# Ordering the start of a four-layer image kernel: the image first, the normalisation as a hand-ordered pipeline, constants and the second image's offsets inside the first gather

## Chip, cores and metric

The kernel runs on one NeuronCore of a Trainium2 chip. The metric is the device time of one execution in microseconds (us); lower is better. All data are float32.

## What is computed

Four layers work one after the other on four images of 192 channels and 64 by 64 pixels. The change concerns the first layer, which, cut to the part that matters, is

```
xn   = layernorm over channels of x            # 192 channels, 4096 pixels
off  = conv3x3(xn, w_p) + b_p                  # 18 offsets for each pixel: 9 taps, x and y
px, py = pixel + tap + off, clipped to the padded image (66 x 66)
xo   = bilinear sample of xn at (px, py)       # 4 neighbours, for 9 taps
att  = channel attention (per head) of conv(xo, w_d)   # its matrices are folded into one 192x192 matrix, m2
x    = x + m2 . xn ;   x = x + mlp(layernorm(x))
```

The second layer is a non-local block over the 4096 pixels, the third is windowed attention with an mlp, the fourth a small depthwise filter.

## The kernel before

All four images go through the same stages. For image b the first layer has three of them.

`offsets(b)` (from line 321) loads the image in eight chunks of 512 pixels (`xi`, L346) and normalises each with the helper `layer_norm_steps` (L271 to L303): mean on TensorE (`pm_l`, L277), difference on VectorE (`d_l`, L281), square on ScalarE (`sq_l`, L284), variance on TensorE (`pv_l`, L256), root on ScalarE (`r_l`, L289), reciprocal on VectorE (L291), spread back over pixels on TensorE (`pb_l`, L265), two products on VectorE (L301) and two affine steps on ScalarE into the padded image `xn` (L302). The helper is a generator, so that a caller can place its steps. Then the 33 tiles of 128 padded pixels are transposed (L372) and copied (`tt`, L373), and each group of 11 tiles is written four times, shifted, into a table in DRAM (`table<-tt`, L376), so that one table row of 3 KB holds a pixel's four neighbours. `xn` itself is written to DRAM too (`xnd`, L379). The 3x3 convolution of `xn` (`po`, L388) runs in three blocks of 4, 4 and 3 groups of 384 pixels, and twelve VectorE steps turn its result into weights and indices (`pos`, `fr`, `idx`, L400 to L417).

`gather(b)` (from L423) is a generator of 297 steps, one for each tile and tap. GpSimd issues an indirect DMA of 128 table rows into one of 11 slots (`ring`, L467); ScalarE and VectorE blend the four neighbours (`row`, `xo`, L473 to L478); TensorE multiplies the result with a tile of `xn` that SyncE loads from the table (`ti`, L463) into the sums `h` (L485). Some twelve short steps on small matrices follow (L501 to L570) and give `m2`. The gather needs the whole table of its image and all of `idx`.

`mlp0(b)` (from L573) reads the image and `xnd` again and applies `m2` and the mlp (L594 to L627).

The order of the stages: constants, `offsets(0)`, `gather(0)`, `offsets(1)`, `mlp0(0)`. Then for each image b come `keys(b)` (L649, eight chunks: load `xk`, two products `tp` L658 and `g` L663) and the second layer `layer1(b)`, with `gather(b+1)` woven into it, and the other layers, with `mlp0(b+1)` woven into them. For b of 1 and 2, `offsets(b+1)` stands between the chunks of `keys(b)`: after each of its eight norms it calls for one chunk.

The constants (L86 to L231) are loaded and prepared ahead of everything else: 48 small copies for one bias table (L141), two weight matrices that are read, scaled and written back to DRAM (`folded`, L181 to L199), and others.

The order on each engine comes from the framework: its scheduler takes the instructions in program order as priority, and lets a later one go ahead where it models it to be ready earlier. Inside `with tc.manual_schedule()` the program order is kept on each engine and on the DMA queue instead. The order is fixed when the program is built; at run time every engine works strictly in order. SBUF that a closed pool held is taken over by later pools, whose first writer waits until the last user is done.

Of the kernel before, what the change touches and what calls it, by code (L numbers as in the profile page):

```python
# [10 lines left out]
F32 = mybir.dt.float32  # L11
# [58 lines left out]
def conv_seq_kernel(ctx: ExitStack, tc: tile.TileContext, a, out: bass.AP):  # L70
# [25 lines left out]
    n128 = sum(m * n for _, m, n in _V128)  # L96
    v128 = load("v128", [128, n128], a["v128"])
    at = 0
    for name, m, n in _V128:
        V[name] = v128[:, at : at + m * n].rearrange("p (m n) -> p m n", m=m)  # L100
        at += m * n

# [14 lines left out]

    thetaT, phiT, gT = halves("thetaT"), halves("phiT"), halves("gT")
    wW = load("wW", [P, C], a["wW"])


    qkvT = const([P + 1, 2, 3 * C], "qkvT")
    nc.sync.dma_start(out=qkvT[:P], in_=a["qkvT"].rearrange("(k p) n -> p k n", p=P))
    nc.sync.dma_start(out=qkvT[P : P + 1, 1, :], in_=a["qkvb"])

    bias = const([128, 3, 2, WS * WS], "bias")


    N1 = 2 * WS - 1
    with tc.tile_pool(name="rpb", bufs=1) as rp:  # L130
        shifted = rp.tile([WS, HEADS, N1 * N1], F32, tag="shifted", name="shifted")
        n = N1 * N1 - WS + 1
        for iy in range(WS):
            nc.sync.dma_start(
                out=shifted[iy : iy + 1, :, 0:n],
                in_=a["rpb"][:, WS - 1 - iy : WS - 1 - iy + n].unsqueeze(0),
            )
        for e in range(HEADS):
            for ix in range(WS):
                rows = shifted[:, e, :].rearrange("p (r c) -> p r c", c=N1)[:, WS - 1 - ix : 2 * WS - 1 - ix, 0:WS]  # L140
                nc.sync.dma_start(out=bias[WS * ix : WS * ix + WS, e % 3, e // 3, :], in_=rows)  # L141
    nc.sync.dma_start(out=bias[64:128], in_=bias[0:64])

    v48 = load("v48", [48, 4], a["v48"])
# [22 lines left out]
    headsel = const([128, 2, P], "headsel")  # L167
    nc.gpsimd.memset(headsel, 0.0)
    for h in range(2):
        for e in range(3):  # L170
            row = P + 2 * e + h
            nc.sync.dma_start(out=headsel[row : row + 1, h, bass.ts(e, 32)], in_=ones[0:1, 0:32])


    sel6 = const([128, 32], "sel6")
    for c in range(0, 32, HEADS):
        n = min(HEADS, 32 - c)
        nc.sync.dma_start(out=sel6[P : P + HEADS, c : c + n], in_=ident[0:HEADS, 0:n])


    def folded(name, gamma, beta, bias_):  # L181

        n = a[name].shape[1]
        to = dram.tile([P, 2, n], F32, tag=f"scaled_{name}", name=f"scaled_{name}")
        b2 = const([128, n // 128], f"bias_{name}")
        with tc.tile_pool(name="fold", bufs=1) as fp, tc.tile_pool(name="foldps", bufs=1, space=PSUM) as pp:
            w = fp.tile([P, 2, n], F32, tag="w", name=f"w_{name}")
            nc.sync.dma_start(out=w, in_=a[name].rearrange("(k p) n -> p k n", p=P))
            p = pp.tile([128, n // 128], F32, tag="p", name=f"p_{name}")
            for m in range(n // 128):  # L190
                for k in range(2):
                    nc.tensor.matmul(
                        p[:, m : m + 1], lhsT=w[:, k, bass.ts(m, 128)], rhs=beta[:, k], start=k == 0, stop=k == 1
                    )
            nc.vector.tensor_tensor(b2, p, bias_.rearrange("p m n -> p (m n)"), ALU.add)
            for k in range(2):
                nc.vector.tensor_scalar_mul(w[:, k, :], w[:, k, :], gamma[:, k])
            nc.sync.dma_start(out=to, in_=w)
        return to, b2  # L199

    fc1_dram, fc1_bias = folded("fc1", V["l0_g2"], V["l0_b2"], V["l0_bfc1"])
    fc1b_dram, fc1b_bias = folded("fc1T", V["l2_n2g"], V["l2_n2b"], V["l2_fc1b"])
    with tc.tile_pool(name="foldq", bufs=1, space=PSUM) as pp:
        p = pp.tile([128, 2, 512], F32, tag="p", name="p_qkv")
        n = 3 * C // 2
        for u in range(2):
            for k in range(2):
                nc.tensor.matmul(
                    p[P : P + 1, u, 0:n], lhsT=V["l2_n1b"][:, k], rhs=qkvT[:P, k, bass.ts(u, n)], start=k == 0, stop=k == 1
                )  # L210
        row = qkvT[P : P + 1, 1, :].rearrange("p (u n) -> p u n", u=2)
        nc.vector.tensor_tensor(row, row, p[P : P + 1, :, 0:n], ALU.add)
        for k in range(2):
            nc.vector.tensor_scalar_mul(qkvT[:P, k, :], qkvT[:P, k, :], V["l2_n1g"][:, k])
# [9 lines left out]


    outb = const([P, 2], "outb")
    with tc.tile_pool(name="outb", bufs=1, space=PSUM) as pp:
        p = pp.tile([P, 2], F32, tag="outb", name="pob")
        for h in range(2):
            nc.tensor.matmul(p[:, h : h + 1], lhsT=wW[:, bass.ts(h, P)], rhs=V["l1_gb"], start=True, stop=True)  # L230
        nc.vector.tensor_tensor(outb, p, V["l1_Wb"].rearrange("p k n -> p (k n)"), ALU.add)  # L231
# [37 lines left out]
    MEAN, DIFFERENCE, SQUARE, VARIANCE, INVERSE = range(5)  # L269

    def layer_norm_steps(src, n, dst, sb, ps, name, affine=None, rows=None, tag="v", bufs=2, own=""):  # L271
# [21 lines left out]
        pb = spread_quarters(r, n, P, ps, name)  # L293
        for k in range(2):
            of, to, r = d[:, k, :], dst[:, k] if rows else dst[:, k, :], pb
            if rows:
                of, r = (t.rearrange("p (r c) -> p r c", r=rows) for t in (of, r))
            if affine is None:
                nc.vector.tensor_tensor(to, of, r, ALU.mult)  # L299
            else:  # L300
                nc.vector.tensor_tensor(of, of, r, ALU.mult)  # L301
                nc.scalar.activation(to, of, AF.Identity, bias=affine[1][:, k], scale=affine[0][:, k])  # L302
        return dst  # L303

    def links(steps, upto=None):

        while True:
            try:
                if next(steps) == upto:
                    return None  # L310
            except StopIteration as end:
                return end.value
# [8 lines left out]
    def offsets(b, pool, beside=None):  # L321
# [18 lines left out]
        with ExitStack() as s:  # L340
# [3 lines left out]
            for i in range(NCH):  # L344
                xi = sb.tile([P, 2, CN], F32, tag="xi", name=f"xi_{b}_{i}")
                nc.sync.dma_start(out=xi, in_=given(b)[:, :, bass.ts(i, CN)])  # L346
                layer_norm(
                    xi, CN, xnv[:, :, 1 + 8 * i : 9 + 8 * i, 1:65], sb, ps, f"l0_{b}_{i}",
                    affine=(V["l0_g1"], V["l0_b1"]), rows=8,
                )  # L350
                if beside is not None:
                    beside()

            wp = s1.tile([P, 2, 9, 32], F32, tag="wp", name=f"wp_{b}")
            nc.gpsimd.memset(wp, 0.0)
            for k in range(2):
                nc.sync.dma_start(out=wp[:, k, :, 0:18], in_=a["wp"][P * k : P * k + P])
            bp = s1.tile([128, 1], F32, tag="bp", name=f"bp_{b}")
            nc.gpsimd.memset(bp, 0.0)
            for q in range(4):  # L360
                nc.sync.dma_start(out=bp[32 * q : 32 * q + 18, :], in_=a["bp"])
            p0 = s1.tile([128, NT, 18], F32, tag="p0", name=f"p0_{b}")
            nc.sync.dma_start(out=p0, in_=a["p0"])

            G, T = 11, 3
            for g in range(NT // G):
                tt = sb.tile([128, G, C], F32, tag="tt", name=f"tt_{b}_{g}")
                for j in range(G):
                    t0 = (g * G + j) * 128 + MID
# [3 lines left out]
                    nc.scalar.copy(tt[:, j, :], pt)  # L373
                for q in range(4):
                    e = g * G * 128 + (2 - q // 2) * WP + 2 - q % 2
                    nc.sync.dma_start(  # L376
                        out=table[e : e + G * 128, bass.ts(q, C)].rearrange("(j p) c -> p j c", p=128), in_=tt
                    )
            nc.sync.dma_start(out=xn_drams[b % 2], in_=xn)  # L379
            for g0 in range(0, NT // T, 4):  # L380
# [3 lines left out]
                for tap in range(9):  # L384
                    for k in range(2):
                        for q in range(ng):
# [4 lines left out]
                            )  # L391
                ot = sb.tile([128, T * 128], F32, tag="ot", name=f"ot_{b}_{g0}")
# [10 lines left out]
                )  # L403

# [15 lines left out]
    def gather(b, s, at, m2):  # L420
# [8 lines left out]
        wkT, wvT, wv, wprojT = (halves(n, keep) for n in ("wkT", "wvT", "wv", "wprojT"))  # L429

        def long(name):

            n = a[name].shape[1]
            lo, hi = (keep.tile([128, n], F32, tag=f"{name}_{i}", name=f"{name}_{i}_{b}") for i in range(2))
            nc.sync.dma_start(out=lo, in_=a[name][64:C])
            nc.sync.dma_start(out=hi[64:128], in_=a[name][0:64])
            return lo, hi

        wk_long, wv_long = long("wkT"), long("wvT")

        wd = keep.tile([128, 14, C], F32, tag="wd", name=f"wd_{b}")
# [1107 lines left out]
```

## Time and profile before

| | |
|---|---|
| time, median of 3 runs | 7646.15 us (7644.78 to 7667.4) |
| time of the profiled execution | 7584.17 us |
| its span | 7582.4 us |
| mean granted TensorE clock | 0.914 |
| TensorE busy | 6609.8 us (87%) |
| VectorE, ScalarE, GpSimd busy | 68%, 49%, 27% |
| constants until the first norm's matmul | 0 to 87.6 us |
| first gather: first and last indirect DMA issued | 191.2 and 614.5 us |
| first matmul of the first image's mlp (`h`, L620) | 726.1 us |
| second layer's first score (`s`, L710) for images 1 and 2 (0 is the first) | 2776.4 and 4544.6 us |

Times in views of the profile are microseconds from the start of the span. A window's row gives, for each engine, its busy time and instruction count, then the granted TensorE clock as a part of full speed, the busy share of the 16 DMA engines, and the GB/s that they moved. In a timeline and in the chain of waits a row is start, duration, and what it was; "<-" stands between what is written and what is read; "SPq" is a DMA issue on SyncE's queue, and an entry "x4" merges four.

### The profile page before, as it was taken

The page shows a single profiled execution, that of the slowest core. Times are in us where ns is not written, and L with a number is a line of the kernel's source. Part 1 is how long each engine was busy: PE and PEld are TensorE (multiplying, and loading weights), DVE is VectorE, ACT ScalarE, POOL GpSimd, SP SyncE. Part 2 cuts the span into 40 slices and gives each one's busy share as a digit, 9 for nine tenths or more (in the row PEclk, how much of TensorE's full clock was granted, in tenths as well). Part 3 has the DMA queues.
Part 4 walks back from the last instruction along what each step waited for, and adds up shares of the span by engine and source line. Part 5 has one row for each costly group of instructions (what it writes and reads, how often), then busy time and mean ns, then how long its engine had stood idle before and what let it go on. Part 6 is the DMA issues. An engine that isn't in the chain of part 4 may idle for free.

```text
span 7582.4 us, 114456 instructions
## 1 busy us (share of the span) xinstructions
PE 6609.8 (87%) x44384; PEld 4281.5 (56%) x44384; DVE 5137.6 (68%) x7998; ACT 3717.0 (49%) x6080; POOL 2084.8 (27%) x2305
## 2 busy tenths in 40 slices
PE   5678999999978789998978879998987879989875
PEld 2455378885534358886634347886643447766432
DVE  2673269974677849994585748995576767755666
ACT  1673258864433248884543327884543325545331
POOL 0671047742100017771200006773210000012100
PEclk9879979997989889998989989998998979999987
DMA  4996147741000166761010056673010010010000
GB/s 136 310 335 211 40 153 222 218 154 33 23 24 13 31 199 216 221 211 50 9 32 17 13 157 218 211 221 110 12 27 22 11 43 11 13 33 10 6 0 18
DMA packets 373069, 756.61 MB, mean 100 GB/s; under 512 B 50999, under 2 KB 253287, under 8 KB 372142
## 3 DMA queue, kind: packets, MB, share of 16 engines
q0 software_dynamic: 95040, 467.22, 19.0%
q1 hardware_dynamic: 277486, 282.08, 12.8%
q8 instruction: 350, 5.73, 0.3%
q14 instruction: 193, 1.58, 0.1%
HBM read 642.66 MB, written 106.21 MB: 99 GB/s over the span
## 4 chain that ended last, share of the span: by engine, by line
PE 69%; DVE 15%; DMA 6%; ACT 5%; issue 2%; SPq 2%; POOL 1%; ACTq 0%; DVEq 0%; POOLq 0%
PE s L710 11%; PE y L776 9%; PE h L485 6%; PE h L1215 5%; PE o L626 3%; PE h L620 3%; DVE ha L1121 3%; PE v L936 3%; DVE ga L1121 2%; DMA ring<-table,idx 2%; PE f L1264 2%; PE qk L861 2%; PE t L944 2%; PE qk L862 2%; PE pm_l2n L277 1%
## 5 line engine op out<-in xcount | busy, mean ns | idle before, releaser
L467 POOL DMA_INDIRECT ring<-table,idx x1188 | 1685.3, 1419 | 1122.4 <-DMA table<-tt 280.5
L710 PE MATMUL s<-ths,ph 96*128 96x256 f32 x4096 | 982.4, 386 | 5.0 <-ACT ths L704 4.0
L710 PEld LDWEIGHTS s<-ths,ph 96*128 96x128 f32 x4096 | 785.6, 193 | 144.1 <-ACT ths L704 17.0
L473 ACT ACTIVATE row<-ring,pos 128x384 f32<-128x384 f32 x1188 | 698.8, 610 | 263.2 <-DVE xo L478 186.2
L485 PE MATMUL h<-ti,xo 128*128 128x192 f32 x3168 | 694.0, 354 | 148.7 <-DVE xo L478 58.5
L474 DVE SCALAR_TENSOR_TENSOR row<-ring,fr,row 128x384 f32<-128x384 f32 x1188 | 699.9, 613 | 122.2 <-ACT row L473 113.3
L776 PE MATMUL y<-sc,gx 128*97 128x256 f32 x3008 | 723.3, 379 | 0.0
L485 PEld LDWEIGHTS h<-ti,xo 128*128 128x128 f32 x3168 | 571.0, 204 | 256.0 <-DVE xo L478 142.3
L1121 DVE SCALAR_TENSOR_TENSOR ga<-gate,v,ga 128x512 f32<-128x512 f32 x720 | 541.4, 752 | 27.6 <-POOL gate L1095 0.2
L776 PEld LDWEIGHTS y<-sc,gx 128*97 128x97 f32 x3008 | 489.6, 164 | 123.3 <-issue 1.1
L477 ACT ACTIVATE xo<-row,pos 128x192 f32<-128x192 f32 x1188 | 505.4, 448 | 76.7 <-PE h L485 60.6
L478 DVE SCALAR_TENSOR_TENSOR xo<-row,fr,xo 128x192 f32<-128x192 f32 x1188 | 465.3, 411 | 55.2 <-ACT xo L477 52.0
L773 DVE TENSOR_TENSOR sc<-sc,mbs 128x1024 f32<-128x1024 f32 x376 | 448.6, 1217 | 12.8 <-ACT mbs L736 12.4
L712 ACT COPY sc<-s 128x1024 f32<-128x1024 f32 x376 | 377.2, 1003 | 158.4 <-PE s L710 157.7
L620 PE MATMUL h<-d_l0m,fc 96*128 96x512 f32 x768 | 375.4, 642 | 86.7 <-DVE d_l0m L299 86.7
L717 DVE TENSOR_TENSOR top<-top,sc 128x1024 f32<-128x1024 f32 x282 | 344.6, 1222 | 127.3 <-ACT sc L712 127.2
L774 ACT ACTIVATE sc<-sc 128x1024 f32<-128x1024 f32 x376 | 393.1, 1054 | 30.5 <-DVE sc L773 28.1
L1095 POOL COPY gate<-gate 128x192 f32<-128x192 f32 x28 | 15.3, 545 | 1397.1 <-ACT gate L1246 1397.1
L920 DVE TENSOR_REDUCE es<-ex 128x6 f32<-128x384 f32 x264 | 133.2, 546 | 391.7 <-ACT ex L916 391.7
L626 PE MATMUL o<-gl,fc 128*96 128x512 f32 x768 | 372.8, 637 | 0.0
L1215 PE MATMUL h<-d_l2n,fc1T 96*128 96x512 f32 x768 | 358.2, 615 | 14.5 <-ACT z L1218 7.8
L620 PEld LDWEIGHTS h<-d_l0m,fc 96*128 96x128 f32 x768 | 157.6, 207 | 294.5 <-issue 186.4
(308 smaller groups left out, 11178.5 us busy)
## 6 DMA issues: line engine op xcount, KB each, us to landing
table<-tt SPq DMA_DIRECT2D x48, 1056.0 KB
ti<-table SPq DMA_DIRECT2D x528, 96.0 KB
ring<-table,idx POOLq DMA_INDIRECT x1188, 5.2
xnd<-xn SPq DMA_DIRECT2D x4, 3270.0 KB
xo<-table SPq DMA_DIRECT2D x132, 96.0 KB
xb<-xnd SPq DMA_DIRECT2D x32, 396.0 KB
xi<-in_x_dram SPq DMA_DIRECT2D x32, 384.0 KB
xa<-in_x_dram SPq DMA_DIRECT2D x32, 384.0 KB
```

The costliest lines, as they stand in the source:

```text
L467: nc.gpsimd.indirect_dma_start(out=gt.rearrange("p r q c -> p (r q c)"), out_offset=None, in_=table[:, :], in_offset=bass.IndirectOffsetOn ...
L473: nc.scalar.activation(row, gt[:, :, 0, :], AF.Copy, scale=pos[:, t, 9 + tap : 10 + tap])
L474: nc.vector.scalar_tensor_tensor(row, gt[:, :, 1, :], fr[:, t, 9 + tap : 10 + tap], row, ALU.mult, ALU.add)
L477: nc.scalar.activation(xo[:, j, :], row[:, 0, :], AF.Copy, scale=pos[:, t, tap : tap + 1])
L478: nc.vector.scalar_tensor_tensor(xo[:, j, :], row[:, 1, :], fr[:, t, tap : tap + 1], xo[:, j, :], ALU.mult, ALU.add)
L485: nc.tensor.matmul(acc[m // 2][:, bass.ts(m % 2, C)], lhsT=xo.rearrange("p j c -> p (j c)")[:, bass.ts(m, 128)], rhs=tt, start=t == 0 and ...
L620: nc.tensor.matmul(p, lhsT=fc1[:, k, bass.ts(m, 128)], rhs=hn[:, k, :], start=k == 0, stop=k == 1)
L626: nc.tensor.matmul(p, lhsT=fc2[:, m, bass.ts(h, P)], rhs=gl[:, m, :], start=m == 0, stop=m == 5)
L710: nc.tensor.matmul(p[:, t, :], lhsT=ph[:, bass.ts(G * g + t, 128)], rhs=ths[i], start=True, stop=True)
L776: nc.tensor.matmul(py, lhsT=gx[:, G * g + t, :], rhs=ex[:, t, :], start=g == 0 and t == 0, stop=g == NG - 1 and t == G - 1,)
L1121: nc.vector.scalar_tensor_tensor(to, src(tap), w[:, k, tap : tap + 1], last, ALU.mult, ALU.add)
L1215: nc.tensor.matmul(p, lhsT=fc1b[:, k, bass.ts(m, 128)], rhs=hns[i][:, k, :], start=k == 0, stop=k == 1)
```

## The change

It has four parts.

1. The constants become a generator `constants()` of eleven yields. Only one small vector table, the identity and a few filled tiles stay in front.
2. `offsets` becomes a generator. For images 0, 2 and 3 it runs in a hand-written order in which the steps of chunk i+1 and chunk i alternate, transposes follow two chunks behind the mean, a third of the first convolution block is placed in each of three steps, and the other two blocks come last; `xnd` is written behind the table's last part. The two products of a norm become one instruction over 1024 elements.
3. While `gather(0)` runs, from its step 30 on, every fourth step takes one part of `constants()`, and after these every sixth step one part of `offsets(1)`, which is left to the scheduler. The loads of the gather's weights move behind its first 66 steps.
4. `keys(1)` and `keys(2)` give one chunk at each yield of `offsets`, which has two yields in each step of its pipeline.

```diff
-    (constants: v128, thetaT, phiT, gT, wW, qkvT, bias, v48, headsel, sel6, folded x2, outb: straight code)
+    def constants():
+        nonlocal thetaT, phiT, ...
+        (the same code, with a yield behind wW, behind each of the six heads of bias, behind headsel,
+         and around each of the two folded())
...
+        if affine is not None:
+            nc.vector.tensor_tensor(d, d, pb.unsqueeze(1).to_broadcast([P, 2, n]), ALU.mult)
+            yield PRODUCT
         for k in range(2):
...
-                nc.vector.tensor_tensor(of, of, r, ALU.mult)
                 nc.scalar.activation(to, of, AF.Identity, bias=affine[1][:, k], scale=affine[0][:, k])
...
+            def ready(i):
+                return NT if i == NCH else max(0, (8 * i + 1) * WP - MID) // 128
+            with ExitStack() as order:
+                if not woven:
+                    order.enter_context(tc.manual_schedule())
+                load(0)
+                load(1)
+                load_weights()
+                norm(0, SQUARE)
+                first = convolve(0)
+                for i in range(NCH + 1):
+                    if i + 2 < NCH:
+                        load(i + 2)
+                    norm(i + 1, MEAN)
+                    norm(i, VARIANCE)
+                    norm(i + 1, DIFFERENCE)
+                    norm(i, INVERSE)
+                    norm(i + 1, SQUARE)
+                    norm(i - 1)
+                    yield
+                    transposes(range(ready(i - 1), ready(i)))
+                    if i >= 5:
+                        next(first, None)
+                    norm(i, PRODUCT)
+                    yield
+                nc.sync.dma_start(out=xn_drams[b % 2], in_=xn)
+                links(first)
+                for g0 in (4, 8):
+                    for _ in convolve(g0):
+                        yield
...
-        for _ in gather(0, s, offsets(0, sb), m2):
-            pass
-        at = offsets(1, second)
+        at = links(offsets(0, sb))
+        beside = [constants(), offsets(1, second, woven=True)]
+        for k, _ in enumerate(gather(0, s, at, m2)):
+            if k < 30 or not beside:
+                continue
+            if len(beside) == 2 and k % 4 == 0 or len(beside) == 1 and k % 6 == 0:
+                try:
+                    next(beside[0])
...
                 if 0 < b < B - 1:
-                    at = offsets(b + 1, sb, lambda: next(making, None))
+                    parts = offsets(b + 1, sb)
+                    try:
+                        while True:
+                            next(parts)
+                            next(making, None)
```

`load`, `load_weights`, `norm(i, upto)`, `transposes` and `convolve` hold the code of before in functions; `convolve` yields after every three taps, and the difference tile `d_l` has three buffers instead of two.

## Prediction

> **What bounds the kernel now.** I read the page first, then the windows, then the chain of waits and the timelines of the three places that the diff touches: the start, the first gather with what follows it, and the offsets of images 2 and 3 beside the keys of images 1 and 2. Everything after the first score of each image's second layer keeps its code, so I sum only up to that point.
>
> Windows of the start and of the first gather:
>
> ```profile
> core 0: us, PE busy (x) PEld busy (x) DVE busy (x) ACT busy (x) POOL busy (x), PEclk, DMA share, GB/s
> 0.00:88.00 88.00, 15.71 (x61) 12.35 (x62) 4.36 (x10) 1.28 (x1) 5.64 (x33) 1.00 0.26 57
> 300.00:400.00 100.00, 72.92 (x344) 52.59 (x342) 83.11 (x171) 81.75 (x173) 75.61 (x73) 0.87 0.95 331
> 2640.00:2666.00 26.00, 24.45 (x75) 15.18 (x74) 16.65 (x20) 2.73 (x4) 0.00 (x0) 0.52 0.38 117
> ```
>
> For 88 us nothing is busy: the constants pass one by one through SyncE's queue. The gather is different: no engine is full, but the DMA engines are, at 0.95.
>
> Chain of waits, start and end of that part:
>
> ```profile
> 55.55 5.17 DMA w_fc<-in_fc_dram
> 87.58 3.71 PE pm_l L277 x4
> ...
> 180.32 9.71 DMA table<-tt
> ...
> 678.51 11.79 PE po L388 x144
> 691.51 11.78 PE po L388 x108
> ```
>
> The first norm begins at 87.58, the table lands at 190.03, the gather starts at 191.2. Behind it the second image's last two convolution blocks stand in the path, 678.5 to 703.3.
>
> Issues of SyncE's queue where image 2's offsets begin, and the DMA view of 190 to 610:
>
> ```profile
> 2634.24 1.22 SPq L655 DMA_DIRECT2D xk<-xd  x2
> 2653.66 8.46 SPq L655 DMA_DIRECT2D xk<-xd  x2
> 2662.18 0.59 SPq L1370 DMA_DIRECT2D out_dram<-out  x1
> 2667.90 0.82 SPq L346 DMA_DIRECT2D xi<-in_x_dram  x2
> DMA packets 49582, 135.27 MB, mean 322 GB/s; under 512 B 7369, under 2 KB 29311, under 8 KB 49550
> ```
>
> The image's first chunk is issued only when the last output of the image before has landed (2662.18 and 5.59, the chain's row for that transfer, make 2667.77): it takes over its SBUF. Key chunks need no such wait and fill TensorE from 2638.66 on.
>
> **First gather's start.** The first `xi` load goes out at about 1.2 instead of 56.0 and lands 5 later (the chain's 5.17 at 2668.28): TensorE starts at 6. The pipeline's step is a loop through three engines, since ScalarE must square chunk i+1 before it may write chunk i-1, whose transposes TensorE then awaits: means 1.72, difference 1.22, square 1.06, two affine steps 1.52, four transposes behind their copies 1.25, spread 1.11, six hand-offs 0.3: 8.2 us. That is what a chunk takes now (126.0 to 134.2), with convolution in its gaps. Chunks before, with few convolution matmuls beside them, took 9.4 (108.1 to 117.5). I take 9.0. The one product of 1024 elements, 1.22 by the difference's row against 1.28 for the two it replaces, gives nothing. The sum: first chunk, cold and with its activation table load, 12.8 (87.6 to 99.7 now, and a slow second mean); four steps of 9.0; three steps of 8.2 with a third of a block, 3.9, in them, 36.4; last product, affine steps, five transposes and an eviction 5.5; two blocks of 11.8 with their evictions 24.9; three adds and nine index instructions with hand-offs 6.9 (2763.5 to 2770.3 for image 2 now). Together 122.5; the gather can start at 129 (126 to 140), 62 earlier. Its table, written from about 97 on with 20 us for the last part (165 to 190 now), comes before that.
>
> **First gather's length.** By the trace it issues its last gather at 614.5, and its products go on up to 633; I take 632 as its natural end, since image 1's transposes and convolution, placed ahead of the last twelve products, hold these until 650.8. The whole DMA load moved inside now is 12 table writes of 1056 KB (13.0 MB), `xnd` 3.3, and constants of 3.3 (four transfers of 576 KB, 432, four of 72, smaller ones) with position tables 0.4: 20 MB, at 322 GB/s 62 us. Nothing hides it, as the share is 0.95 already. Beside it SyncE's queue gets about 85 small issues of 0.7, eight bias copies (5.5 us) for every four gather steps (5.5 us at 1.37 each), and table writes that hold the queue (18.3 us for four at 165.0); `ti` loads queue behind them, and TensorE's `h` behind those. The ring's 11 slots cover 15 us. I take 20 for what is left, ends 0 and 45. The moved weights cost the same bytes. So the last products end at 129 + (632 - 191) + 62 + 20 = 652.
>
> **Behind it.** The small matrices take 27.4 now (651.5 to 678.9), of which 5.5 are image 1's: 22. The mlp's loads are now hidden by the convolution that goes away: about 3 of issue and 5 of landing become visible, and from the first `m2` product (704.9) to the first `h` of the mlp (726.3) it is 21.4 as before. 652 + 22 + 8 + 21.4 = 703.4, against 726.3: **23 earlier** (ends, with the start at 126 to 140 and the weave at 0 to 45: 46 earlier, 13 later). The 25 us of convolution that leave the path give back only part: the loads and first norm of the mlp are late next.
>
> **Images 2 and 3.** Here the hand-written order adds a wait. Queued on TensorE behind the first mean are all eight key chunks; on SyncE `xk` stands behind the third `xi` load, which awaits the first difference. Now five and a half chunks run before the first mean (2673.5), in a time when TensorE has nothing else. After the change TensorE idles there. The last output instruction ends at 2656.1; without `xk` ahead of it its store lands at 2661.7, and `xi` at 2667. From there: first step 19 (the first difference ends 5 behind `xi`, `xk` lands 4 later, two key chunks of 3.64, the first slow, 8.9, spread 1.1); three steps of 8.2 less the 3.3 idle now filled, plus 7.3 of keys, 12.2 each, 36.6; one of 9; three with convolution 36.4; then 5.5, 24.9 and 6.9 as above; 6.1 from the index to the first score (2770.3 to 2776.4). 144.4: the score starts at 2811.4, not 2776.4, **35 later**. For image 3 the same with 4417.65, so `xi` at 4428.5: 4572.9 against 4544.6, **28 later**. Ends for both together: if `xi` need not wait and goes out with `xk` (2634.2, 4395.8, and 5.2 to land), 7 and 1; if it comes when it does now (2673.5, 4440.1), 42 and 40. I take 63, since the conflict is in the trace twice and the pool of `xi` becomes larger, not smaller.
>
> On the clock: 2640 to 2666 TensorE was 94% busy at a granted 0.52, and at 2666 it had full speed. The Trainium skill ("TensorE: Matmul & The Clock Gate", What's actually happening) says full rate comes after about 3.4 us of sustained work. By the rule my first steps are short enough as they stand; by the row the half clock could go on for 26 us and each of the two stages would be about 8 longer.
>
> **Sum.** 63 - 23 = 40 later. The profiled execution took 7584.2 with its span of 7582.4, so 7624 in its terms. The median of the runs shown is 62 above it; in the runs' terms 7646 + 40 = **7686**.
>
> **Rivals.** (1) *The loads are not held.* If the other SBUF layout lets `xi` go out with `xk`, images 2 and 3 lose 8 together, and with a clean weave (0 instead of 20) the first part gains 43: 35 faster, 7611. It decides as soon as the two stages cost less than the start gives. For it: weights and biases (L357 to L363) are in SBUF at 2616 already. Against: two of two waits. (2) *The moved bytes are hidden.* If the first gather were bound by VectorE and ScalarE (0.83 and 0.82 at 300 to 400), 62 would vanish and the 20 with them: 42 faster, 7604. Against: from 400 to 600, with those at 0.66 to 0.74, the pace is 1.31, hardly less than 1.37, and the DMA share the same. (3) *The weave stalls the gather.* Each load behind a blocked SyncE queue comes late, and a matmul on image 1 that awaits one blocks `h`, as for 39.9 us once at the start (wait of `h` for `xi`). If a third of 24 parts lose 8 us, it is 44 more: 84 slower, 7730. (4) *It does not do what it says:* the scheduler is free for image 1 and may push its parts behind the gather again, as now. Then the start gains its 62, the tail stays, the constants' 3.7 MB add 11, and the two stages 63: 12 slower, 7658.
>
> **Chances.** Forecast, including (4), 0.58, spread over +5 to +75 us; 0.11 of it within 0.3%, that is 23 us, about what a measurement of this kernel can tell from no change. Rival (1) 0.27, 0.24 of it faster by more. Rival (2) 0.08, faster. Rival (3) 0.07, slower. So faster 0.32, same 0.14, slower 0.54. The range reaches below rivals (1) and (2), and up to the forecast with the upper ends of the two stages (82 instead of 63), the weave (45) and the start (140): 7600 to 7740. The forecast's own: 7651 to 7721.
>
> **What would show it.** Right: first norm's matmul at 6 to 8, first indirect DMA at 126 to 140, DMA share still 0.95 and the gather some 80 longer, `h` of the mlp near 703; between 2627 and 2667 an idle TensorE, `tp` only after `pm_l`, first scores 30 later than now, counted from the end of the image before. Wrong: key chunks before the first mean of images 2 and 3, or a gather of 440 us with the tables inside it.

## The result and the profile after

The changed kernel is slower: 7736.94 us against 7656.77 (medians of 4 runs each), a ratio of 1.0115 with a 95% interval of 1.0087 to 1.0143, so 80 us where 40 were forecast. Its profiled execution spans 7730.8.

These numbers need one caution. The runs fall into two groups, A and B. In A the kernel before has medians of 7567 to 7582, in B of 7657 and 7678. The record numbers the chips: all later runs of group A are from chips 1, 8 and 11, all of group B from chip 2, in one series. The first comparison has no number; it is of group B by its runs, but the profiled execution of before (7584.2) is like those of group A. The changed kernel once more in B gave 1.0098 (1.006 to 1.0136), in A 1.0159 (1.0121 to 1.0197), which is 64 and 110 us. I therefore take the stages from two profiles made on one chip in A, spans 7549.8 and 7673.5. The last column is the version with no order by hand (`e8_again` below), also in A.

| stage, us | forecast change | before | after | change | no order by hand |
|---|---|---|---|---|---|
| span's start to first gather | -62 | 191.9 | 164.2 | -28 | 113.1 |
| first gather, to its last `h` | +63 | 450.3 | 524.0 | +74 | 522.6 |
| on to the first `h` of the mlp | -24 | 75.3 | 58.6 | -17 | 56.0 |
| image 2: first output store to first score | +35 | 154.5 | 208.1 | +54 | 146.5 |
| image 3: the same | +28 | 154.8 | 204.5 | +50 | 146.7 |
| all the rest | 0 | 6523.0 | 6514.1 | -9 | 6541.2 |

The forecast changes of the first three rows are 129 - 191.2, 652 - 129 - 459.6 and 703.4 - 652 - 75.3, against the first profile.

Windows of the changed kernel's first profile, in the columns of the prediction: the start in two parts, the same 100 us of the gather, and the place of image 2.

```profile
core 0: us, PE busy (x) PEld busy (x) DVE busy (x) ACT busy (x) POOL busy (x), PEclk, DMA share, GB/s
0.00:33.00 33.00, 9.79 (x33) 4.54 (x34) 4.60 (x4) 4.93 (x5) 5.58 (x33) 0.72 0.50 145
33.00:98.00 65.00, 45.00 (x236) 22.96 (x238) 16.67 (x15) 20.33 (x40) 0.00 (x0) 0.62 0.35 98
...
300.00:400.00 100.00, 80.21 (x491) 52.61 (x489) 70.69 (x133) 72.19 (x159) 67.02 (x64) 0.89 0.98 322
2650.00:2687.00 37.00, 0.00 (x0) 0.03 (x1) 27.98 (x32) 0.00 (x0) 0.16 (x1) 0.54 0.41 119
2687.00:2765.00 78.00, 56.30 (x301) 35.71 (x302) 18.40 (x20) 19.24 (x35) 0.00 (x0) 0.78 0.44 126
```

The gather is DMA-bound as forecast (0.98 in these 100 us, 0.91 over the whole gather in A), and TensorE idles 37 us before image 2's first mean as forecast. What the forecast does not have is in the rows 33 to 98 and 2687 to 2765: once the norms run, no engine is full and the DMA engines are at 0.35 and 0.44, so something else sets the pace.

From SyncE's queue in the first 34 us of that profile (start, length, instruction; "x4" merges four):

```profile
10.97 0.40 SPq L256 DMA_DIRECT2D table<-zero  x1
11.47 12.18 SPq L372 DMA_DIRECT2D wp<-in_wp_dram  x2
23.75 4.15 SPq L375 DMA_DIRECT2D bp<-in_bp_dram  x4
27.95 0.35 SPq L376 DMA_DIRECT2D p<-in_p_dram  x1
28.40 0.86 SPq L367 DMA_DIRECT2D xi<-in_x_dram  x2
```

And its chain of waits (start, length, what) at four places: the third and the seventh mean of image 0, the end of the gather, and a step of image 2.

```profile
28.40 3.97 DMA xi<-in_x_dram
...
32.50 3.70 PE pm_l L289 x4
...
66.28 3.31 SPq L406
...
69.68 10.11 DMA xi<-in_x_dram
...
79.84 3.73 PE pm_l L289 x4
...
714.96 8.76 PE h L554 x49
...
724.27 9.86 PE pg L570 x56
...
2744.95 3.30 SPq L406
...
2748.35 9.62 DMA xk<-xd
...
2758.10 3.70 PE tp L727 x4
```

TensorE has nothing else from 17 us on (idle 15.24 before the mean at 32.50), but the third `xi` is issued behind the convolution's weights, biases and positions, which hold the queue until 28.3. Later loads stand behind the four table writes (L406), and so does the eighth key chunk of image 2, for which TensorE waits 16.8 us. The convolution blocks that stood in the chain at 678.5 and 691.5 are gone from there: `pg` follows the last `h` at once.

### The profile page after: what moved, and what is told of

Its sections match the earlier page's. It is cut to its first block, busy times and chain, and to the rows that moved or that the text cites. A ratio compares the mean times of both kernels' runs of the same rounds, so it can differ in the third digit from the quotient of the medians.

```text
span 7730.8 us, 114407 instructions
## 1 busy us (share of the span) xinstructions
PE 6624.1 (86%) x44384; PEld 4294.4 (56%) x44384; DVE 5130.7 (66%) x7966; ACT 3709.6 (48%) x6080; POOL 2071.7 (27%) x2305
## 4 chain that ended last, share of the span: by engine, by line
PE 69%; DVE 15%; ACT 5%; DMA 5%; issue 3%; POOL 1%; SPq 1%; another core or an unknown queue 1%; ACTq 0%; DVEq 0%; POOLq 0%
PE s L779 11%; PE y L845 10%; PE h L554 6%; PE h L1284 4%; PE o L695 3%; PE h L689 3%; DVE ha L1190 3%; PE v L1005 3%; DVE ga L1190 2%; PE po L419 2%; PE f L1333 2%; PE qk L930 2%; PE t L1013 2%; PE qk L931 2%; PE pm_l2n L289 1%
## 5 line engine op out<-in xcount | busy, mean ns | idle before, releaser
L554 PE MATMUL h<-ti,xo 128*128 128x192 f32 x3168 | 687.1, 356 | 153.3 <-DMA ti<-table 83.1
L542 ACT ACTIVATE row<-ring,pos 128x384 f32<-128x384 f32 x1188 | 693.5, 608 | 219.1 <-DVE xo L547 146.5
```

Source lines behind the costliest of these rows:

```text
L542: nc.scalar.activation(row, gt[:, :, 0, :], AF.Copy, scale=pos[:, t, 9 + tap : 10 + tap])
L554: nc.tensor.matmul(acc[m // 2][:, bass.ts(m % 2, C)], lhsT=xo.rearrange("p j c -> p (j c)")[:, bass.ts(m, 128)], rhs=tt, start=t == 0 and ...
```

## The experiments

**Where a stage's time lies.** For the three places I split the time at the first and the eighth mean (`pm_l`); the last part runs to the first gather for image 0, to the first score for images 2 and 3. The forecast's row is its own sum, cut there: 6.0, then 12.8 + 36 + 12.1, then the rest up to 129; for the others 2667 - 2628.4, then 19 + 36.6 + 9 + 12.1, then the rest of 144.4.

| kernel | image 0 | image 2 | image 3 |
|---|---|---|---|
| before (beside after, A) | 87.6 + 63.7 + 40.6 | 50.0 + 59.2 + 45.3 | 50.1 + 59.2 + 45.5 |
| forecast | 6.0 + 60.9 + 62.1 | 38.6 + 76.7 + 67.7 | 38.6 + 76.7 + 67.7 |
| after (A) | 5.2 + 91.3 + 67.7 | 36.0 + 104.2 + 67.9 | 35.6 + 102.6 + 66.4 |
| e2_keys5 (B) | 5.2 + 91.9 + 67.8 | 46.5 + 83.6 + 68.6 | 46.7 + 81.1 + 66.3 |
| e3_weights_late (B) | 5.6 + 87.6 + 67.6 | 35.6 + 102.7 + 66.8 | 35.3 + 102.7 + 66.5 |
| e6_xi_pool (B) | 11.9 + 67.1 + 67.4 | 36.5 + 97.0 + 68.6 | 36.6 + 96.4 + 68.6 |
| e12_both_pool (A) | 11.9 + 68.8 + 67.7 | 36.7 + 83.1 + 68.8 | 36.5 + 81.3 + 66.7 |
| e13_both_pool_keys5 (A) | 11.9 + 66.9 + 67.4 | 40.2 + 74.0 + 66.8 | 47.2 + 76.5 + 67.7 |
| e1_free23 (A) | 5.8 + 89.5 + 67.4 | 50.1 + 45.2 + 51.3 | 49.8 + 45.0 + 51.4 |
| e8_free_all (A) | 5.1 + 63.2 + 43.5 | 44.7 + 43.8 + 51.0 | 44.2 + 43.6 + 51.1 |
| e8_again (A) | 5.3 + 64.4 + 43.5 | 50.0 + 45.3 + 51.3 | 50.2 + 45.2 + 51.3 |
| e9_free_seq (A) | 5.2 + 78.0 + 41.2 | 49.7 + 63.7 + 46.0 | 44.4 + 62.3 + 46.3 |
| e10_free_pool (A) | 5.2 + 53.5 + 49.9 | 49.7 + 45.1 + 50.2 | 44.2 + 43.6 + 50.9 |

**The kernel before again** (no edit), for its stages and their spread.

> The kernel before once more, for a second profile of it. The first profile ended at 7582.4, some 70 below the kernel's own other runs, while the changed kernel's profile stood level with its other runs; so the 148 between the two profiles is larger than the 80 between the medians. Theory 1, the granted clock: one image's window stage is 278 instead of 264 in a profile, in another image each time; then this profile has its stages within 3 of the first one's everywhere but in such a place, and an end anywhere from 7580 to 7670. Theory 2, the stages that the change touches differ from run to run themselves: then the gather of 459.6 and the starts of images 2 and 3 (148.0 and 154.7 from the first output store to the first score) move by 10 or more.

> The kernel before, for a profile on the same chip as the three kernels beside it. On one chip (medians of the kernel before 7582) its first gather took 454.2 and that of a kernel with the changed head 518.7; on another (medians 7678) the changed head's took 554 to 564 in five kernels, and the kernel before has no profile there. Theory: a slower chip lengthens both alike, so that the difference of the two on one chip is 60 to 70, wherever it is; on a chip like the second the kernel before shows about 495. Rival: the added load alone is slower there, and the kernel before shows 455 to 460 on either.

> The kernel before, beside the changed kernel on one chip, both with a profile. Theory: the changed kernel's gather is about 65 longer than this one's on any chip, and images 2 and 3 about 56 and 51 longer, so that the difference is near 115 on a chip like that of 7567 to 7582. Rival: the cost of the gather depends on the chip; on one like that of 7657 to 7678, this kernel's gather is then 530 or more, within 30 of the changed kernel's 560.

> The kernel before once more, for its stages on whichever chip this falls on. On the chip of 7567 to 7582 its first gather took 450 to 454 in three profiles, beside 519 to 524 with the changed head. If it falls on the slower one (medians 7657 to 7678), where the changed head took 554 to 564: by the theory that the chip lengthens both alike, 485 to 500; by the rival that the difference itself depends on the chip, 530 or more.

All four fell in group A: spans 7558.5, 7560.4, 7549.8 and 7565.7. The gather took 454.2, 452.7, 450.3 and 454.8, image 2's stage 147.7 to 154.6, image 3's 154.1 to 154.9. So the touched stages repeat within 5 to 7. That is between the theories. Elsewhere single stretches move by up to 15 (the mlp up to the first score 269.6 to 283.1; image 0's windows up to its first output store 898.0 in the first profile, 883.2 to 885.2 in these). The sum of all the rest, as in the table of stages, lies between 6523.0 and 6553.5 in the five profiles of the kernel before, and between 6514.1 and 6576.2 in all kernels here. A gain of 20 to 30 in one stage is therefore read from the stage and not from the length of one execution. The kernel before never got a profile in group B, so whether its gather is longer there too stays open.

**The changed kernel again** (no edit).

> The changed kernel once more. With the order by hand taken out of images 2 and 3 alone, the first gather lasted 518.7, though nothing was edited there; constants alone beside it made it 486.4, the second image alone 491.6, neither 459.7 or 454.2: 32 and 37 more, which add up to 523. The 560.2 of the changed kernel's first profile does not fit. Theory 1 (the runs of that profile had a slower gather, and nothing else): it lasts 515 to 525 here, and the first product of the mlp comes 40 earlier than in that profile, near 735; images 2 and 3 keep 205 to 209 from first output store to first score, and the ratio to the kernel before is about 1.015 still. Theory 2 (the layout of buffers differs with the order): 555 to 565 again.

> The changed kernel beside the kernel before on one chip. Its median stood 64 to 80 above the kernel before on the chip of 7657 to 7678. By stages measured on the other chip (head 12 later, images 2 and 3 56 and 51) it should stand 105 to 120 above there, near 7685, ratio 1.014 to 1.016, with a gather of 515 to 525. If the gather is 555 or more on the faster chip too, the order by hand of the later images lengthens it, and the ratio is 1.02.

The first fell in B (gather 560.9, ratio 1.0098), the second in A (524.0, 1.0159). The gather's length thus goes with the group, at the same instructions, and not with the order by hand of later images. The two ratios' intervals overlap, so that the change costs less in B is not shown.

**The order by hand: only for image 0** (`e1_free23`).

```
-                if not woven:
+                if b == 0:
                     order.enter_context(tc.manual_schedule())
```

> The hand-written order is kept for the first image alone; images 2 and 3 keep the pipeline of norms, but the scheduler places their instructions. Theory (the order written by hand costs all of it: key chunks behind the first mean, loads behind weights and table writes in SyncE's queue): from first output store to first score 148 and 155 again instead of 208.7 and 205.3, the end 111 earlier, about 7626, ratio 0.996 of the kernel before. Rival (the pipeline of single steps or the larger pool of differences costs it, however it is ordered): both stages stay above 190 and the end within 30 of 7737. Between the two (170 to 190), the scheduler follows the written order as a priority and part of the loss is in that.

Measured 7567.71, ratio 0.9982 (0.9964 to 1.0); the stages took 146.6 and 146.1. The theory holds: the 54 and 50 lost come back, and in image 3, whose stage before repeats within 1 us, 8 more. The first mean comes 14 later, behind the keys, and everything behind it is faster.

**Keys first** (`e2_keys5`): `for _ in range(5): next(making)` ahead of the loop over `parts`.

> As the changed kernel, but the first five key chunks of images 1 and 2 stand ahead of the next image's offsets, so that they run while the first xi is awaited; three stay between the steps. Theory (idle TensorE before the first mean, and keys in every step, are what was lost): five chunks of 3.6 to 7.3 leave the steps, so first output store to first score falls from 208.7 and 205.3 to 180 or less. Rival (SyncE's queue in the order of the text, weights and table writes ahead of loads, is the larger part): it stays above 190, since the loads still stand behind the same writes.

198.7 and 194.1, ratio 1.0093 (1.0064 to 1.0121) beside 1.0098 for the changed kernel in the same series: the rival. The steps lose 21, but the first mean comes 11 later, since the last output store now stands behind `xk` loads again. The idle TensorE that the prediction put first is worth 6 to 11 net.

**Weights later** (`e3_weights_late`).

```
                 load(1)
-                load_weights()
...
                         load(i + 2)
+                    if i == 3:
+                        load_weights()
```

> As the changed kernel, but the convolution's weights, biases and positions are loaded behind the sixth chunk's load instead of behind the second's. Theory (they hold SyncE's queue for 17 us, 11.5 to 28.4 in the changed kernel's profile, and the third xi stands behind them): the second step starts 15 earlier and the first gather at 147 to 150 instead of 163. In images 2 and 3 the first xk and third xi stand behind them too: their stages fall by about 10, to 195 to 199. Rival (what follows is the bound anyway: table writes ahead of the later loads): the gather starts at 158 or later, since the same 17 us are only paid at the sixth chunk.

First gather at 160.9, images 2 and 3 205.2 and 204.5, ratio 1.0101 (1.006 to 1.0142): the rival. The third and fourth `xi` were issued from 12.2 on instead of from 28.8, right behind eight transfers of zeros to the tables, and the two issues held the queue for 6.4. TensorE began on the third only at 29.9. From 24 to 30 the DMA share was 0.07, so the end of the wait is not for bandwidth; what it is for is not settled. In the first chunks, then, the weights in the queue are not the only holder.

**The loads on another queue.** `e6_xi_pool` issues `xi` of images 0, 2 and 3 with `nc.gpsimd`; `e12_both_pool` issues the key chunks of images 1 and 2 with it as well; `e13_both_pool_keys5` has the five key chunks ahead in addition.

```
-                nc.sync.dma_start(out=xi, in_=given(b)[:, :, bass.ts(i, CN)])
+                (nc.sync if woven else nc.gpsimd).dma_start(out=xi, in_=given(b)[:, :, bass.ts(i, CN)])
...
-            nc.sync.dma_start(out=x, in_=x_drams[b % 2][:, :, cols])
+            (nc.gpsimd if 0 < b < B - 1 else nc.sync).dma_start(out=x, in_=x_drams[b % 2][:, :, cols])
```

> As the changed kernel, but the xi loads of images 0, 2 and 3 are issued on GpSimd's queue, where nothing else stands at those times; xk, weights and table writes stay on SyncE's. Theory (the loads are late because they stand behind weights and table writes in one queue): no pm_l waits for xi after the first step, the steps take 8.2 to 10 each and the first gather starts at 130 to 138; images 2 and 3 gain too, but xk still stands behind weights and writes: 180 to 195. Rival (xi is late because its buffer comes free late, or the writes fill the DMA engines so that any load beside them is slow): the gather starts at 155 or later.

> As the changed kernel, but the loads of xi (images 0, 2 and 3) and of the key chunks (images 1 and 2) are issued on GpSimd's queue, where no weights or table writes stand. With xi alone there, images 2 and 3 took 202.0 and 201.6, and the eighth key chunk still held TensorE for 20 behind four table writes. Theory (loads behind writes in SyncE's queue are a separate cost of some 30): the stages fall to 165 to 180. Rival (the order by hand on TensorE, ScalarE and VectorE is the cost, wherever the loads wait): they stay above 190.

> As the one with both loads on GpSimd's queue, and five key chunks ahead of the next image's offsets as well. Five chunks ahead alone gave 198.7 and 194.1. Theory (queue and keys add up to the whole): 150 to 160, near the 147 without order by hand. Rival (the steps keep a length of their own under the order by hand): 170 or more.

With `xi` alone the first gather starts at 146.3, although the first mean is 6.7 later; from first to eighth mean it is 67.1 instead of 91.3. That is between theory and rival; the steps give back 24. Images 2 and 3 gave 202.0 and 201.6: less than its theory, because the key chunk stays behind the writes. The whole time does not show this gain: 7753.25, ratio 1.0117 (1.008 to 1.0154), beside 7741.98 and 1.0098 for the changed kernel in the same series. In its profile the first product of the mlp comes 28 earlier, but the untouched rest is 6576.2 against 6546.6, the longest of all profiles; why, no run shows. With both loads moved, 188.6 and 184.4, between its theory and its rival: the steps give back 21 each. This kernel and the next ran once each, 7644.0 and 7626.5, beside 7675.3 for the changed kernel's profiled run on that chip. With the keys ahead too, 181.1 and 191.3: the steps shorten by 9 and 5, but the first mean comes 4 and 11 later, so its rival holds. SyncE's queue in `e12_both_pool`, beside image 2's steps:

```profile
2649.35 0.36 SPq L376 DMA_DIRECT2D p<-in_p_dram  x1
2702.08 7.99 SPq L406 DMA_DIRECT2D table<-tt  x4
```

The writes hold the queue for 8 us as before, but nothing is behind them, and the 31.9 us step of the changed kernel (2699.8 to 2731.7 in its profile of group A) is 11.5 (2694.6 to 2706.1). In all six kernels of the table with the order by hand for these three images, the part behind the eighth mean stays at 66 to 69: as long as forecast in images 2 and 3 (67.7), 5 to 6 longer in image 0 (62.1).

**The two halves of the weave.** `e4_const_front` runs `constants()` before `offsets(0, sb)` and weaves the second image alone; `e5_second_after` weaves the constants alone and makes the second image's offsets behind the gather.

> The constants go back in front of the first image's offsets; the second image's offsets stay woven into the first gather. The gather lasted 459.6 before (first indirect DMA to last product) and 560.2 after. Theory A (the constants' many small issues stall the gather): it falls to 510 or less, since both their 11 us of bytes and their stalls go. Theory B (the second image's table writes do it): it stays at 540 to 550, less by the bytes alone. The first norm comes at about 88 as before, the first gather at about 240, since the loads and weights behind it stand as in the changed kernel; by B the end is about 65 later than the changed kernel's, 7800, by A about 30 later, 7765.

> The constants stay woven into the first gather; the second image's offsets stand behind it in the text, as in the kernel before, with the pipeline of norms and no order by hand. Theory A (constants stall the gather): it lasts 510 or more. Theory B (table writes and the like of the second image do it): it lasts 460 to 485, that is 459.6 with 11 us of bytes and a little more, if the scheduler leaves image 1's table writes behind it as in the kernel before. The mlp's first product then comes 75 behind the last gather product as in the kernel before, instead of 54: under B at 163.8 + 475 + 75 = 714, 64 earlier than in the changed kernel and 12 earlier than in the kernel before.

`e4_const_front`: 7742.9, ratio 1.0215 (1.0192 to 1.0237), first mean at 105.6, gather 491.6. `e5_second_after`: 7661.16, ratio 1.011 (1.0086 to 1.0134), gather 486.4. Both ran in A, while the bounds of the theories were set from a gather of 560.2, which is of group B. Neither theory alone: against 450 to 455, the second image adds about 38, the constants about 33, together 71; both woven gave 518.7 to 524.1. In bytes, the DMA view of the gather up to its last `h`, first before, then after (group A):

```profile
DMA packets 55204, 144.24 MB, mean 321 GB/s; under 512 B 7755, under 2 KB 34530, under 8 KB 55074
```

```profile
DMA packets 76790, 159.94 MB, mean 305 GB/s; under 512 B 11672, under 2 KB 55536, under 8 KB 76656
```

15.7 MB more, at 321 GB/s 49 us; the slower pace, 305, makes the other 25 (159.94 / 305 against 159.94 / 321). But this window of the kernel before ends with four table writes and `xnd` of image 1, issued from 621 on, behind the last indirect DMA (606.8). From the first to the last indirect DMA it moved 136.71 MB in 414.9 us (329 GB/s), the changed kernel 157.66 MB in 504.9 us (312): 21 MB more, which at 329 GB/s is 64 us, and 26 for the pace. The constants' gather moved only 146.56 MB, 2.3 more, but at 301 GB/s: they cost by pace, the second image by bytes (156.59 MB at 318). Whether the pace falls because loads are held or because the constants come in small pieces is not split: the DMA share fell only from 0.94 to 0.91. What is woven must also repay itself: the constants in the gather bring the mlp's first `h` from 791.0 to 734.5 (`e4_const_front` against `e1_free23`, A), while the second image woven in brings it from 723.9 (`e5_second_after`) to 734.5 or 746.8, later.

**No order by hand at all** (`e8_free_all`, and `e8_again`): the two lines of `manual_schedule` are gone. `e9_free_seq` also undoes the pipeline in the text (`load(i)`, `norm(i)` whole, `transposes`), `e10_free_pool` has the weights late and image 0's third to eighth `xi` on GpSimd's queue.

```
-                if not woven:
-                    order.enter_context(tc.manual_schedule())
```

> As the changed kernel, but without any order by hand: image 0, too, is placed by the scheduler. With the order by hand removed from images 2 and 3, these took 146.6 and 146.1 instead of 208.7 and 205.3. Theory (the order by hand costs image 0 the same way: its steps wait at fixed places for loads behind other traffic, with no other work let in between): from first mean to first gather it takes some 105 instead of 158, as in the kernel before (103.6), and the first gather starts at 110 to 125, the mlp 40 to 50 earlier than with the order kept for image 0; the end about 45 below that, ratio 0.990 to 0.993 of the kernel before. Rival (image 0 is bound by its loads and by SyncE's queue, which this leaves): the gather starts at 150 or later and the ratio is 0.996 to 1.0.

> The changed kernel without any order by hand once more, beside that profile. Its ratio to the kernel before was 0.9952, with an interval of 0.9926 to 0.9978. Theory: the gain (first product of the mlp 30 earlier, images 2 and 3 8 and 15 shorter) is there again, ratio 0.993 to 0.997. Rival: it was within the spread of the runs, and 1.0 lies in the interval now.

> As the one beside it without any order by hand, and without the pipeline in the text too: one chunk's norm whole after the other, its transposes behind it. Theory (the scheduler interleaves the chunks by itself, as it did before the change, and the pipeline in the text gives little): images 2 and 3 within 6 of 146, as in the kernel before (148.0 and 154.7), and the end within 15 of the kernel beside it. Rival (the written pipeline is what brought 146 against 155): both 8 or more longer.

> Without any order by hand, and image 0's third to eighth xi are issued on GpSimd's queue; the convolution's weights are loaded behind the sixth chunk. Under the order by hand the queue alone started the gather 19 earlier (146.3 for 165.6), the weights alone 5. Theory (order and queue are separate costs): the gather starts 10 to 25 earlier than in the kernel without order by hand beside it, and the end as much. Rival (without the order nothing waits for the loads): within 5 of it.

`e8_free_all`: 7523.43, ratio 0.9952 (0.9926 to 0.9978), first gather at 111.8 and the mlp 44 earlier than in `e1_free23`, as its theory has it, but the end gains less than the theory's ratio. `e8_again`: 7531.47, 0.9948 (0.9927 to 0.9968). This version beats the kernel before by half a per cent. `e9_free_seq`: 7565.44, 1.0002 (0.9981 to 1.0024), images 2 and 3 at 159.4 and 153.1, which is the rival: the pipeline in the text is worth half a per cent, if the scheduler may place it. `e10_free_pool`: 7527.24, 0.9945 (0.9922 to 0.9968): its means end 10 earlier, but the part behind them is 6 longer, and the rival holds; without the fixed order the loads' queue is hardly in the path. Windows of `e8_again`, then of the changed kernel in A, from the third mean on:

```profile
33.00:68.00 35.00, 34.67 (x267) 16.84 (x266) 16.76 (x15) 18.66 (x38) 0.00 (x0) 0.92 0.60 173
```

```profile
33.00:98.00 65.00, 45.20 (x232) 22.77 (x230) 16.67 (x15) 20.35 (x40) 0.00 (x0) 0.61 0.35 98
```

The third mean is as late in both (32.1 and 32.5). But where the scheduler places them, TensorE is busy 34.7 of 35 us at a granted 0.92, with more matmuls than in the 65 us of the fixed order at 0.61.

## Why the prediction was wrong in size and right in direction

- **The failed step is the pipeline's steps: "8.2 us. That is what a chunk takes now ... I take 9.0"**, with 12.2 and 12.1 for those with keys and convolution. By its own sum, from the first to the eighth mean 60.9 and 76.7 were forecast; it took 91.3, 104.2 and 102.6, or 30, 28 and 26 more. The loop through three engines was priced, the loads that feed it were not: in the order by hand, SyncE's queue runs weights, table writes and loads as the text has them. Image 0's first step took 27.3 for 12.8, with the weights ahead of the third load, and the one that ends with the seventh mean 16.2 for 9.0, behind table writes; in image 2, 20 of the 28 lie in the one step of 31.9 for 12.2. Moved to another queue the loads give back 24 in image 0 and 21 each in images 2 and 3. So the queue is shown as the larger part. The last 5 to 8 are steps that are longer without it: in `e12_both_pool` image 0's steps without convolution took 10.1 to 10.9 for 9.0, the first with it 15.6 for 12.1. What makes them longer is open; the lower clock is a candidate that no run isolates.
- **The start: "the gather can start at 129".** 164.2 in A, 163.8 in the first profile. The first mean (6 forecast, 5.1 and 5.2 measured) was right; 30 of the 35 are the step above, 5.6 the part behind the eighth mean, where the two whole convolution blocks took 28.0 (129.7 to 157.7) for 24.9.
- **The gather: 652 - 129 = 523.** 524.0, 518.7, 524.1 and 522.6 in A; 553.5 to 564.2 in B, where I can't say what the kernel before takes. The mechanism was right: from the first to the last indirect DMA it became 90 longer in A, 64 by bytes and 26 by pace, for 62 and 20, and the products behind the last one took 19.2 instead of 35.4, as forecast. That the length fits to 1 us is luck: the last indirect DMA came 423.3 behind the first in the profile that the forecast began from, 414.9 in A, which makes up for the 8 by which bytes and pace were larger. The bytes, too, are partly other ones: the second gather's weights, 2.2 MB, came in at 529 to 547 (at 696 to 703 before), which the forecast doesn't have.
- **Behind it: 51.4.** 58.6 in A, 54.3 in the first profile.
- **Images 2 and 3: "the hand-written order adds a wait".** Right in kind: `tp` comes only after `pm_l`, TensorE idles, and without the order five and a half key chunks run ahead of the first mean again. 35 and 28 were forecast, 54 and 50 measured (61 and 51 between the first two profiles). The first mean was right within 3 us (38.6 against 36.0) and the part behind the eighth mean to 0.2 (67.7 against 67.9), the steps between were not. And the named wait, key chunks held back, is the smaller piece: running five of them ahead gives 6 to 11.
- **The clock.** The forecast left the rule and the row side by side. Before image 2's first mean in the kernel before, the window in group A reads:

```profile
2600.00:2639.00 39.00, 37.45 (x104) 23.22 (x103) 18.64 (x23) 3.41 (x5) 0.00 (x0) 0.50 0.44 131
```

  TensorE is 96% busy for 39 us at half clock. The Trainium skill ("TensorE: Matmul & The Clock Gate", What's actually happening) gives full rate after about 3.4 us of sustained work; this row, like the prediction's, does not agree, and the measurement decides. In the changed kernel (A) the granted clock was 0.76 from 2653 to 2666, where image 2's first step begins, 0.68 from 2666 to 2679, though TensorE was busy for all of it, and 1.00 from there to 2707. That step took 23.3 instead of 19; how much of the 4.3 is the clock is not shown.
- **The rivals.** (1) `xi` without a wait: no, it was issued 4.4 behind the last output's store. (2) Hidden bytes: no, +74. (3) The weave stalls the gather: at most the 26 of pace, and not 64. (4) The scheduler pushes image 1 behind the gather: no, its norms ran at 311.8 to 404.3, its table writes at 363.7 to 483.4. None of the four has SyncE's order in the steps, though the prediction itself counted 18.3 us in which four table writes hold that queue, and used it for the weave alone.

## What to carry to other kernels

An order written by hand fixes every engine's queue, the one that issues transfers too: list what stands in it ahead of each load that a pipelined step waits for, and price it step by step. Write the pipeline in the text and let the scheduler place it; in group A that alone turned 1.6% slower into 0.5% faster. What is woven into a DMA-bound stage pays its bytes there, so weave only what was exposed before (the constants, for which nothing ran up to 87.6), not what already ran beside other work; the free order with the second image's offsets behind the gather was not tried.

## What the runs showed of the hardware

- A second issuing queue saved much more than the issue. The Trainium skill ("DMA: Bandwidth & Descriptors", Issuing engines are not separate DMA queues) says that issuing on several engines only saves the sequencer's time, usually small beside the transfer. With `xi` and `xk` on GpSimd's queue, 24 us of one stage and 21 of two others went, since an in-order queue held by writes (7.7 us for four in the changed kernel, 12.2 for two weight loads) keeps back loads that transfer in 4 alone and in 10 beside table writes.
- In image 0's norms the granted clock was 0.61 where TensorE was busy 45 of 65 us, 0.92 where it was 34.7 of 35. Gaps alone do not set it: it was 0.50 where TensorE was busy 37.45 of 39 us.
- The same instructions in the same order moved at 305 GB/s in group A and 286 in group B (159.94 MB in 524.0 us; a gather of 560.2), which makes 36 us of one stage.
